# Two-layer graph network on one core: the first gathers' wait on the copy of x rows, the place of both layers' scatters behind the last gather, and layer 1's results in the own rows' places

## The chip, the cores and the metric

The kernel runs on one core of one Trainium2 chip. The metric is the device time of one execution in microseconds. The core has five engines: PE (matmul), DVE (vector work), ACT (scalar functions), POOL (here mostly the issuer of indirect DMAs) and SP (the issuer of most plain DMAs). Transfers themselves run on 16 DMA engines.

## The reference

A graph of N = 3327 nodes with F = 512 features each, all in f32. The adjacency matrix is symmetric with ones on the diagonal, and a row has some nine nonzeros on average (each pair is drawn at 0.0024). Both layers end in a residual and a layernorm.

```python
# layer 0: attention over neighbours, 4 heads of 128
feats = einsum('nf,hfo->hno', x, W)
logits = leaky_relu(e_self[:, :, None] + e_neigh[:, None, :], 0.2), masked by A
out0 = relu(concat over heads of softmax(logits) @ feats + b)
x = layernorm(x + out0)
# layer 1: two gated sums over the same neighbours
h = x @ W_sa;  s_left, s_right = h @ a_sa[:F], h @ a_sa[F:]
gate_a = sigmoid([A @ x, x] @ Wa.T + ba);  gate_b likewise with Wb
e = exp(-leaky_relu(s_left[:, None] + s_right[None, :], 0.01)) where A != 0, else 0
out1 = sigmoid(gate_a * (e / (sum(e) + 1e-5)) @ h + gate_b * (A @ (x @ W_g) + b_g))
x = layernorm(x + out1)
```

## The kernel before

The 3327 nodes are padded to 26 tiles of 128 rows. `sparse_pass` does not multiply by the adjacency matrix. It turns the matrix into lists of neighbours, sorts the nodes by their number of neighbours, and then fetches, for each tile, the neighbours' rows with indirect DMAs (a "gather": 128 rows of 2080 bytes, one row for each partition). A tile needs as many gathers as its longest list (the constant `CAPS`, 4 to 14), and nodes with still longer lists get an extra slot. The nodes form two groups: the first 12 tiles and the other 14. `gat_then_gated_gnn` calls `sparse_pass`, and after it a dense version that runs only if the graph doesn't fit the lists, which is not the case here.

**Up to about 200 us: lists and features.** The adjacency matrix comes in seven chunks on SP's queue (`load_adj`, L222). PE packs it into codes (L403), DVE takes the largest codes and decodes them (L71, L74, L442 to L479). Beside that, PE computes each tile's rows of features (L372), ACT copies them, and POOL sends them to a table in DRAM, `table0` (L384). The rows of the first group's nodes alternate in this table with their rows of x, so that one gather of double width gets a node's own features and its own x. These rows of x are copied into the table by one DMA of SP, `x_rows` (L238), which is put just ahead of the last adjacency chunk.

**About 200 to 632 us: layer 0, tile by tile.** `plan` writes down a tile's gathers in the list `waiting`, each with the number of slots handed out up to it. `gather` issues them on POOL (`indirect`, L616) from the head of that list as long as they fit into the `ring`, 42 slots of 128 rows in SBUF. `free(j)` gives a tile's slots back in program order. `at_first` issues, ahead of everything else, those gathers of the two tiles `early` that read features only (11 in all), and puts their two double-width gathers behind them. For each tile DVE and ACT then compute the softmax weights (`weigh_a`, L750 to L763, `weigh_b`, L777 to L779), DVE and ACT scale the gathered rows (L798, L796), and PE adds them up with a matmul by the identity (`attend`, L804). DVE adds the residual (`finish`, L883), the columns that layer 1 needs are worked out (L835, L839), and after each group of tiles `Norm` yields the layernorm's scale and shift. `publish` normalises a tile's row (ACT) and its columns (DVE, L846 and L847). It stays in SBUF as `row1(j)` and goes to the table of layer 1, `table1`: the first group's tiles by a plain DMA of SP (L849), the second group's by an indirect DMA of POOL (`put_rows`, which calls `scatter`, L146), since their order in DRAM is another one.

**About 632 to 1077 us: layer 1.** All gathers of layer 1 are planned at once, and a loop over the 26 tiles issues them by `gather` as slots come free. DVE computes weights (L1031 to L1061) and the weighted sum (`weighted`, L1096 and L1098), PE the plain sum (`plain_sum`, L1117), turns both (L1127) and multiplies them by the two weight matrices (`project`, L1136). Two steps later DVE forms the argument of the sigmoid in a buffer `za` (L1166), ACT takes its tanh (L1168), and DVE adds the residual `row1` (L1190). When `Norm` has a group (it ends at the tiles 3, 7, 11, 15, 19, 22, 24 and 25 of the order), ACT normalises its tiles in place (L1183) and POOL sends each to its place in the output (`scatter`, L146).

Instructions of one engine run in the order of the program. So a scatter that waits for ACT holds up the gathers behind it on POOL. A buffer of a pool with several copies (`bufs`) can be written again only once its last reader, a scatter's DMA among them, has finished. The framework derives all these waits from the regions that instructions read and write. Two helpers take a wait out: `declare_no_dep` opens a named group with one instruction in it, and `add_to_no_dep_group` adds an instruction to an existing group. `scatter` uses the groups `table1` and `out` so.

Of the kernel before, what the change touches and what calls it, by code (L numbers as in the profile page):

```python
# [8 lines left out]
F32 = mybir.dt.float32  # L9
AF = mybir.ActivationFunctionType  # L10
ALU = mybir.AluOpType
# [3 lines left out]
P = 128  # L15
# [20 lines left out]
GRP = 4  # L36
# [42 lines left out]
def sparse_pass(  # L79
# [39 lines left out]
    nc = tc.nc  # L119
    N, F = out.shape  # L120
# [23 lines left out]
    def scatter(group, dst, rows, src, last=None):  # L144

        put = nc.gpsimd.indirect_dma_start(  # L146
            out=dst, out_offset=bass.IndirectOffsetOnAxis(ap=rows, axis=0), in_=src, in_offset=None,
            bounds_check=last, oob_is_err=last is None,
        ).ins
        tc.declare_no_dep(put, group=group, reason="their rows are disjoint")  # L150
        tc.add_to_no_dep_group(group, put)
        nc.gpsimd.nop(nofuse=True)
# [23 lines left out]
    def place(j):  # L176

        return (0, j) if j < NG[0] else (1, j - NG[0])

    def own(j):  # L180
        g, i = place(j)
        return srt[g][:, i, 0:1]

    def row1(j):
        g, i = place(j)
        return x1[g][:, i, :]
# [22 lines left out]
    def load_x(i):  # L209
        if i < len(chunks):  # L210
            cw = min(CH, NP - chunks[i])
            xc = xcs[i] = pj.tile([P, KT, CH], F32, tag="xc", name=f"xc{i}", bufs=3)
            nc.sync.dma_start(xc[:, :, :cw], xB[i] if cw == CH else xL)
# [4 lines left out]
    def load_adj(i):  # L218
        cw = min(CH, NP - chunks[i])
        for q, (a, b) in enumerate(pairs_of(NT)):  # L220
            at = p0.tile([P, 2, CH], F32, tag="at", name=f"at{i}_{a}", bufs=AT)
            nc.sync.dma_start(at[:, :, :cw], adjB[i, q] if cw == CH else adjL[q])  # L222

            ones_of = at.bitcast(BF16).rearrange("p t (n w) -> p t n w", w=2)[:, :, :cw, 1]
            loaded[i, a], loaded[i, b] = ones_of[:, 0], ones_of[:, 1]
# [10 lines left out]
    for i in range(len(chunks)):  # L236
        if i == len(chunks) - 1:
            x_rows = nc.sync.dma_start(twos.rearrange("(n t) w -> n t w", t=2)[:, 0, :], xo[:N0]).ins  # L238
            tc.declare_no_dep(x_rows, group="x rows", reason="the first gathers read rows of features only")
        load_adj(i)  # L240
        load_x(i + 2)

# [370 lines left out]
    waiting, ends_at = [], {}  # L613

    def indirect(out_, table, ap):
        return nc.gpsimd.indirect_dma_start(  # L616
            out=out_, out_offset=None, in_=table, in_offset=bass.IndirectOffsetOnAxis(ap=ap, axis=0)
        ).ins
# [42 lines left out]
    def free(j):  # L661

        freed[0] = ends_at[j]
# [68 lines left out]
    first = list(range(NG[0]))  # L732
# [94 lines left out]
    def columns2a(j):  # L827
        xt1s[j] = m0.tile([P, KT, P], F32, tag="xt1", name=f"xt1_{j}")
        nc.scalar.copy(xt1s[j], turned[j])
# [8 lines left out]
    def columns3(j):  # L838
        nc.vector.tensor_copy(row1(j)[:, F : F + NCOL], turned[j])  # L839

    def publish(j, scale, shift):
        row = row1(j)[:, 0:F]
        nc.scalar.activation(row, row, AF.Identity, scale=scale, bias=shift)
        col = row1(j)[:, F : F + NCOL]
        t = m0.tile([P, NCOL], F32, tag="shifted", name=f"shifted{j}")
        nc.vector.scalar_tensor_tensor(t, v1sum, shift, bias8, ALU.mult, ALU.add)  # L846
        nc.vector.scalar_tensor_tensor(col, col, scale, t, ALU.mult, ALU.add)  # L847
        if j < NG[0]:
            put = nc.sync.dma_start(table1[j * P : (j + 1) * P, :], row1(j)).ins  # L849
            tc.add_to_no_dep_group("table1", put)  # L850
        else:
            rows_ready.append(j)
# [3 lines left out]
    def put_rows():  # L856
        for j in rows_ready:
            scatter("table1", table1[:, :], own(j), row1(j), N - 1)
        rows_ready.clear()
# [14 lines left out]
    def at_first():  # L874

        a, b = (CAPS[j] + 1 for j in early)
        waiting[: a + b] = waiting[1:a] + waiting[a + 1 : a + b] + [waiting[0], waiting[a]]
        for _ in range(a + b - 2):
            tc.add_to_no_dep_group("x rows", indirect(*waiting.pop(0)[1:]))

    def finish(j):
        y = row1(j)[:, 0:F]
# [64 lines left out]
    ready = [[], []]  # L947
    for i in range(NT + 3):
        for args in ready[0]:
            publish(*args)  # L950
        ready = [ready[1], []]
        third = order0[i - 2] if 2 <= i < NT + 2 else None
        if third is not None:
            columns2a(third)
        if 2 <= i < NT:
            attend(order0[i], i >= 3, lambda: third is None or columns2(third))
        elif third is not None:
            columns2(third)
        if 0 < i <= NT:
            j = order0[i - 1]  # L960
            y = row1(j)[:, 0:F]
            if i > 2:
                finish(j)
            put_rows()
            columns1(j)
            done = norm.add(i - 1, y)
            if done:
                k0, scale, shift = done
                ready[1] = [
                    (order0[k], scale[:, k - k0 : k - k0 + 1], shift[:, k - k0 : k - k0 + 1]) for k in range(k0, i)  # L970
                ]
        if i > NT:
            put_rows()
        if 2 <= i < NT + 2:
            columns3(order0[i - 2])
        if 0 < i <= 7:
            sort1(rankis[1], 2 * i - 2, 2 * i)
        if i == 8:
            climb(1, m0, psx.tile([P, B * H], F32, tag="pcol", name="climb1", bufs=2)[:, : B + H])
        if i == NG[0]:  # L980
            nc.vector.memset(over, 0.0)
            for j, c in enumerate(CAPS):
                if j in T0:
                    nc.vector.tensor_scalar(over[:, j, c:S], no_step, 0.0, None, ALU.is_lt)
                else:
                    nc.vector.memset(over[:, j, c:S], 1.0)
        if i == 3:
            nc.sync.dma_start(own1[:, 0, :], xo[N0:])
            nc.sync.dma_start(own1[:, 1, :], singles)
        if 2 <= i < NT - 1:  # L990
            weigh_a(order0[i + 1])
            weigh_b(order0[i + 1])
# [6 lines left out]
    m1 = ctx.enter_context(tc.tile_pool(name="m1", bufs=2))  # L999
# [8 lines left out]
    order, last, mid = by_len[2:7], by_len[:2][::-1], by_len[7:]  # L1008
# [7 lines left out]
    ew, gates, sums, plain, proj, zs, stair_sum = {}, {}, {}, {}, {}, {}, {}  # L1016
# [128 lines left out]
    weights_a(at_(0))  # L1145
    weights_b(at_(0))
    scaled_first(at_(0))
    ready = None
    for i in range(NT + 3):
        j, j1, jp, jpp = at_(i), at_(i + 1), at_(i - 1), at_(i - 2)  # L1150
        if i > 0 and jp is not None:
            free(jp)
        gather()
        if j1 is not None:
            own_score(j1)
        if jp is not None:
            sp = zs[jp, "sp"] = m1.tile([P, F], F32, tag="sp", name=f"sp{jp}")
            nc.scalar.activation(sp, plain[jp], AF.Copy, scale=gates[jp][:, 1:2])
            turn(jp, 0)
            turn(jp, 1)  # L1160
        if j is not None:
            plain_sum(j, False)
            weighted(j, 0)
        if jpp is not None:
            za = zs[jpp] = m1.tile([P, F], F32, tag="za", name=f"za{jpp}", bufs=GRP + 3)
            nc.vector.scalar_tensor_tensor(za, bias_g, gates[jpp][:, 1:2], proj[jpp], ALU.mult, ALU.add)  # L1166

            nc.scalar.activation(za, za, AF.Tanh, scale=0.5)  # L1168
        if jp is not None:
            project(jp, 0)  # L1170
        if j is not None:
            plain_sum(j, True)
        if j1 is not None:
            weights_a(j1)
        if j is not None:
            weighted(j, 1)
        if jp is not None:
            project(jp, 1)
        if ready:
            k0, scale, shift = ready  # L1180
            for k in range(k0, i - 2):
                z = zs[order[k]]
                nc.scalar.activation(  # L1183
                    z, z, AF.Identity, scale=scale[:, k - k0 : k - k0 + 1], bias=shift[:, k - k0 : k - k0 + 1]
                )
                scatter("out", out, own(order[k]), z, N - 1)
            ready = None
        if jpp is not None:
            za = zs[jpp]
            nc.vector.scalar_tensor_tensor(za, za, 0.5, row1(jpp)[:, 0:F], ALU.mult, ALU.add)  # L1190
        if j1 is not None:
            weights_b(j1)
            scaled_first(j1)
        if jpp is not None:
            ready = norm.add(i - 2, zs[jpp])
# [452 lines left out]
```

## Time and profile before

| What | us |
|---|---|
| Runs | 1079.59, 1087.12, 1090.84 |
| Median of the runs | 1087.12 |
| The profiled execution's own time | 1079.52 |
| Its span in the profile | 1077.4 |
| Last row of features sent by POOL | 157.63 |
| First gather of layer 0 issued | 177.22 |
| Last gather of layer 0 issued | 583.62 |
| Last scatter of layer 0 issued | 628.53 |
| Last gather of layer 1 issued | 994.68 |
| Last scatter of layer 1 issued | 1070.61 |

Times inside the profile are counted from the start of the span. A row of the costliest groups reads: line, engine, operation, output<-inputs and count, then busy time and mean ns of one, then the idle time that the engine had just before these instructions, with what ended most of it. The DMA_INDIRECT on POOL is the issue of a gather or scatter; the data lands later. A row of a timeline reads: start, duration, engine, line, operation, and in brackets the idle time before it with its releaser. A row of the waits reads: engine and line, what it waited for, then the total, the number of times, and the longest. A row of the windows gives, for each stretch, its length and each engine's busy time with its instructions, then the granted clock of PE, the share of the DMA engines and GB/s. "issue" is time in which the engine waited for nothing that the profile shows, "remote" a release by something that it can't name.

### The profile page before, as it was taken

Reading aid. Unit: us, or ns where it says so; the run is one execution under the profiler, and the core shown is the slowest. Engines: PE = TensorE matmul, PEld = TensorE weight load, DVE = VectorE, ACT = ScalarE, POOL = GpSimd, SP = SyncE. Lnnn points to the kernel's source line nnn. Section 1 sums busy time; section 2 is a strip of 40 time slices with the busy share of each in tenths; the row PEclk is TensorE's granted clock in tenths of the full one; section 3 lists DMA queues with packets and bytes.
Section 4 is the critical chain, followed back from the end, with each engine's and each line's share of the span. In section 5 each row is a group of like instructions: output and inputs, shape, how many; then the busy total and the mean of one; then the engine's idle time right before and its main releaser. Section 6 shows DMA issues by size and latency. Waiting matters only on the chain. (4 is left out here: it accounts for less than half of the span.)

```text
span 1077.4 us, 10335 instructions
## 1 busy us (share of the span) xinstructions
PE 823.0 (76%) x2518; PEld 431.5 (40%) x2518; DVE 735.3 (68%) x2100; ACT 288.8 (27%) x820; POOL 594.3 (55%) x641
## 2 busy tenths in 40 slices
PE   5698973053978887888588936289999969979994
PEld 4476751022434443434244412044444424434442
DVE  3486788137666676666448846069898986979983
ACT  1122210021333342434135511022223213222331
POOL 7511243752667666576755157755777777767101
PEclk9898995575997988888878967589999998989998
DMA  9999899982568677587765047745676675756101
GB/s 341 374 360 399 329 334 370 395 302 80 167 183 257 200 212 221 180 297 200 207 175 178 31 130 190 214 129 139 177 192 187 175 190 173 193 161 189 49 8 55
DMA packets 73349, 224.68 MB, mean 209 GB/s; under 512 B 12736, under 2 KB 16784, under 8 KB 72384
## 3 DMA queue, kind: packets, MB, share of 16 engines
q0 software_dynamic: 46368, 153.69, 48.2%
q1 hardware_dynamic: 24256, 68.13, 16.7%
q10 hardware_dynamic: 2656, 2.10, 0.6%
q8 instruction: 23, 0.38, 0.1%
q14 instruction: 46, 0.38, 0.1%
HBM read 203.02 MB, written 31.51 MB: 218 GB/s over the span
## 5 line engine op out<-in xcount | busy, mean ns | idle before, releaser
L616 POOL DMA_INDIRECT ring<-table,srt x464 | 475.4, 1025 | 247.7 <-issue 109.3
L804 PE MATMUL acc<-ring,ident 128*128 128x512 f32 x504 | 262.9, 669 | 90.3 <-DMA ring<-table,srt 33.7
L804 PEld LDWEIGHTS acc<-ring,ident 128*128 128x128 f32 x504 | 102.1, 213 | 215.2 <-issue 146.3
L1096 DVE SCALAR_TENSOR_TENSOR sw<-ring,e,sw 128x512 f32<-128x512 f32 x226 | 169.4, 750 | 12.7 <-ACT sw L1080 7.2
L1117 PE MATMUL acc<-ring,ident 128*128 128x512 f32 x264 | 126.7, 615 | 12.8 <-DMA ring<-table,srt 9.6
L1136 PE MATMUL po<-wsa,sT 128*128 128x512 f32 x208 | 100.0, 627 | 32.0 <-issue 29.1
L372 PE MATMUL pf<-w,xc 128*128 128x260 f32 x416 | 106.0, 419 | 13.1 <-DVE w L312 13.1
L798 DVE TENSOR_TENSOR ring<-ring,w 128x512 f32<-128x512 f32 x176 | 111.3, 691 | 0.5
L372 PEld LDWEIGHTS pf<-w,xc 128*128 128x128 f32 x416 | 86.4, 210 | 30.2 <-DVE w L312 13.8
L1136 PE MATMUL po<-wg,sT 128*128 128x512 f32 x208 | 93.7, 593 | 0.0
L796 ACT ACTIVATE ring<-ring,w 128x128 f32<-128x128 f32 x304 | 91.6, 390 | 0.9 <-issue 0.9
L1117 PEld LDWEIGHTS acc<-ring,ident 128*128 128x128 f32 x264 | 51.7, 197 | 82.0 <-issue 56.9
L1136 PEld LDWEIGHTS po<-wsa,sT 128*128 128x128 f32 x208 | 41.7, 202 | 88.6 <-issue 82.6
L146 POOL DMA_INDIRECT out<-za,srt x26 | 29.1, 1118 | 78.8 <-ACT za L1183 74.6
L1098 DVE TENSOR_TENSOR ring<-ring 128x512 f32<-128x512 f32 x94 | 65.0, 691 | 3.2
L763 ACT ACTIVATE w<-w 128x40 f32<-128x40 f32 (+10 forms) x26 | 6.2, 237 | 212.5 <-DVE w L762 113.6
L384 POOL DMA_DIRECT2D table<-row x26 | 14.3, 549 | 87.4 <-ACT st L381 84.7
L1129 ACT COPY sT<-pt 128x512 f32<-128x512 f32 x52 | 28.5, 588 | 117.9 <-PE pt L1127 57.0
L1136 PEld LDWEIGHTS po<-wg,sT 128*128 128x128 f32 x208 | 39.4, 190 | 48.8 <-issue 47.8
L403 PE MATMUL pc<-at,pow 128*32 128x512 bf16 (+1 forms) x182 | 24.4, 414 | 39.7 <-DMA at<-in_adjB 24.9
L1166 DVE SCALAR_TENSOR_TENSOR za<-bias_g,gate,po 128x512 f32<-128x512 f32 x26 | 19.3, 742 | 38.6 <-remote 29.2
L376 ACT COPY row<-pf 128x512 f32<-128x512 f32 x26 | 15.2, 586 | 97.7 <-issue 49.2
(253 smaller groups left out, 949.9 us busy)
## 6 DMA issues: line engine op xcount, KB each, us to landing
at<-in_adjB SPq DMA_DIRECT2D x78, 512.0 KB
ring<-table,srt POOLq DMA_INDIRECT x464
table<-row POOLq DMA_DIRECT2D x26, 260.0 KB
xc<-in_xB SPq DMA_DIRECT2D x6, 1024.0 KB
own<-in_xo SPq DMA_DIRECT2D x1, 3640.0 KB
own<-table SPq DMA_DIRECT2D x1, 3640.0 KB
at<-in_adjL SPq DMA_DIRECT2D x13, 256.0 KB
table<-in_xo SPq DMA_DIRECT2D x1, 3120.0 KB
```

The lines of the kernel that those rows point to most:

```text
L146: put = nc.gpsimd.indirect_dma_start(out=dst, out_offset=bass.IndirectOffsetOnAxis(ap=rows, axis=0), in_=src, in_offset=None, bounds_check ...
L372: nc.tensor.matmul(pf[:, hh, :HC], xc[:, k, o : o + P], w0[:, k, hh, :], start=(k == 0), stop=(k == KT - 1))
L403: nc.tensor.matmul(pc[32 * c : 32 * c + 32, : nt * P], pow2[:, s, :], loaded[i, m], start=(s == 0), stop=(m + 1 not in ms or s == 3),)
L616: return nc.gpsimd.indirect_dma_start(out=out_, out_offset=None, in_=table, in_offset=bass.IndirectOffsetOnAxis(ap=ap, axis=0)).ins
L796: nc.scalar.activation(gv[:, h, :], gv[:, h, :], AF.Copy, scale=w[:, s, h : h + 1])
L798: nc.vector.tensor_tensor(gv, gv, w[:, s, :].rearrange("p (h o) -> p h o", o=1).to_broadcast([P, H, FO]), ALU.mult)
L804: nc.tensor.matmul(acc, ident, row, start=(lean and s == 0), stop=(s == CAPS[j] and j not in T0))
L1096: nc.vector.scalar_tensor_tensor(sw, g[:, i, 0:F], e[:, s : s + 1], sw, ALU.mult, ALU.add)
L1098: nc.vector.tensor_add(g[:, i, 0:F], g[:, i - 1, 0:F], g[:, i, 0:F])
L1117: nc.tensor.matmul(plain[j], to, row, start=(not sums_of_two and i == 0), stop=(sums_of_two and i == len(rows) - 1),)
L1129: nc.scalar.copy(sT, pt)
L1136: nc.tensor.matmul(proj[j], sT[:, k, :], wt[:, k, :], start=(half + k == 0), stop=(half + k == KT))
```

## The change

There are three parts.

The copy of x rows and the first gathers change their roles in the group `x rows`: each of the 11 gathers of `at_first` is now declared itself, and `x_rows` is added to the group. In the program as compiled before, the first gather waits for the copy `x_rows`. In the program as compiled after, the first gather waits for the rows of features and for a word written into them earlier, and the wait for `x_rows` stands at the twelfth gather, the first of double width.

In layer 0, `put_rows` is called inside the loop only when `waiting` is empty, so when all gathers of layer 0 have been issued. Four of the 14 scatters stood ahead of further gathers before; now all 14 stand behind the last one.

In layer 1, the residual (L1190) writes its result into `row1(j)`, where it read the residual from, and no longer into `za`. ACT normalises it there, and the scatter reads it there. The pool of `za` has three buffers instead of seven. The scatters are collected in a list `outs` and issued once `waiting` is empty. Before, 16 of the 26 stood ahead of further gathers; now all stand behind the last one. The number of instructions is the same on each engine.

```diff
--- before.py
+++ after.py
@@ -236,7 +236,7 @@
     for i in range(len(chunks)):
         if i == len(chunks) - 1:
             x_rows = nc.sync.dma_start(twos.rearrange("(n t) w -> n t w", t=2)[:, 0, :], xo[:N0]).ins
-            tc.declare_no_dep(x_rows, group="x rows", reason="the first gathers read rows of features only")
+            tc.add_to_no_dep_group("x rows", x_rows)
         load_adj(i)
         load_x(i + 2)
 
@@ -876,7 +876,7 @@
         a, b = (CAPS[j] + 1 for j in early)
         waiting[: a + b] = waiting[1:a] + waiting[a + 1 : a + b] + [waiting[0], waiting[a]]
         for _ in range(a + b - 2):
-            tc.add_to_no_dep_group("x rows", indirect(*waiting.pop(0)[1:]))
+            tc.declare_no_dep(indirect(*waiting.pop(0)[1:]), group="x rows", reason="they read rows of features only")
 
     def finish(j):
         y = row1(j)[:, 0:F]
@@ -961,7 +961,8 @@
             y = row1(j)[:, 0:F]
             if i > 2:
                 finish(j)
-            put_rows()
+            if not waiting:
+                put_rows()
             columns1(j)
             done = norm.add(i - 1, y)
             if done:
@@ -1145,7 +1146,7 @@
     weights_a(at_(0))
     weights_b(at_(0))
     scaled_first(at_(0))
-    ready = None
+    ready, outs = None, []
     for i in range(NT + 3):
         j, j1, jp, jpp = at_(i), at_(i + 1), at_(i - 1), at_(i - 2)
         if i > 0 and jp is not None:
@@ -1162,7 +1163,7 @@
             plain_sum(j, False)
             weighted(j, 0)
         if jpp is not None:
-            za = zs[jpp] = m1.tile([P, F], F32, tag="za", name=f"za{jpp}", bufs=GRP + 3)
+            za = zs[jpp] = m1.tile([P, F], F32, tag="za", name=f"za{jpp}", bufs=3)
             nc.vector.scalar_tensor_tensor(za, bias_g, gates[jpp][:, 1:2], proj[jpp], ALU.mult, ALU.add)
 
             nc.scalar.activation(za, za, AF.Tanh, scale=0.5)
@@ -1179,15 +1180,18 @@
         if ready:
             k0, scale, shift = ready
             for k in range(k0, i - 2):
-                z = zs[order[k]]
+                z = row1(order[k])[:, 0:F]
                 nc.scalar.activation(
                     z, z, AF.Identity, scale=scale[:, k - k0 : k - k0 + 1], bias=shift[:, k - k0 : k - k0 + 1]
                 )
-                scatter("out", out, own(order[k]), z, N - 1)
+                outs.append((own(order[k]), z))
             ready = None
+        while outs and not waiting:
+            scatter("out", out, *outs.pop(0), N - 1)
         if jpp is not None:
             za = zs[jpp]
-            nc.vector.scalar_tensor_tensor(za, za, 0.5, row1(jpp)[:, 0:F], ALU.mult, ALU.add)
+            zs[jpp] = row1(jpp)[:, 0:F]
+            nc.vector.scalar_tensor_tensor(zs[jpp], za, 0.5, zs[jpp], ALU.mult, ALU.add)
         if j1 is not None:
             weights_b(j1)
             scaled_first(j1)
```

## The prediction

> **What bounds the kernel now.** I read the page first (engine totals, chain, costliest groups), then each engine's waits, then windows by stage, and last the timelines of POOL and DVE around the places that the change touches.
>
> ```profile
> span 1077.4 us, 10335 instructions
> PE 823.0 (76%) x2518; PEld 431.5 (40%) x2518; DVE 735.3 (68%) x2100; ACT 288.8 (27%) x820; POOL 594.3 (55%) x641
> issue 11%; DVE 10%; PE 8%; DMA 4%; POOL 3%; another core or an unknown queue 3%; ACT 2%; POOLq 0%; DVEq 0%
> L616 POOL DMA_INDIRECT ring<-table,srt x464 | 475.4, 1025 | 247.7 <-issue 109.3
> L146 POOL DMA_INDIRECT out<-za,srt x26 | 29.1, 1118 | 78.8 <-ACT za L1183 74.6
> ```
>
> No engine is full over the whole span. POOL, whose queue the change rearranges, is busy for 55%, and its gathers (L616) are preceded by 247.7 us of idle time: it has room. The windows by stage say what fills each:
>
> ```profile
> core 0: us, PE busy (x) PEld busy (x) DVE busy (x) ACT busy (x) POOL busy (x), PEclk, DMA share, GB/s
> 150.00:205.00 55.00, 21.26 (x100) 10.65 (x98) 37.87 (x170) 3.07 (x10) 23.55 (x27) 0.60 1.04 377
> 260.00:632.00 372.00, 302.14 (x842) 150.00 (x842) 243.06 (x712) 141.08 (x418) 215.02 (x216) 0.85 0.61 185
> 660.00:700.00 40.00, 11.10 (x26) 4.89 (x24) 7.33 (x14) 1.49 (x3) 30.25 (x33) 0.66 0.75 208
> 700.00:800.00 100.00, 94.54 (x257) 45.40 (x258) 83.15 (x184) 27.71 (x68) 63.99 (x59) 0.95 0.56 157
> 900.00:1000.00 100.00, 92.51 (x249) 43.51 (x248) 89.06 (x185) 25.59 (x65) 71.66 (x66) 0.95 0.63 176
> ```
>
> Layer 0 (260 to 632) is PE work (81%), layer 1 (700 to 1000) PE and DVE together (94% and 83%, then 93% and 89%). Before 205 the DMA engines are full. The stretch 660 to 700 is odd: PE, DVE and ACT nearly stand still while POOL issues gathers.
>
> Then the question that decides this change: does anybody wait for a gather? Among DVE's waits over the whole span, one row is for the ring that the gathers fill:
>
> ```profile
> DVE za L1166 <- remote: 29.2, 2, 24.9
> DVE e L1031 <- DMA ring<-table,srt: 12.2, 2, 11.5
> ```
>
> The 11.5 us is the start of layer 1 (at 641 us), which waits for layer 0's last scatter at 628.5, itself waiting for DVE. In DVE's waits from 660 to 1000 no row names the ring. Taking each gather's issue against its first reader in the timelines, I find its data landed 15 us or more ahead in layer 0, and 20 us or more in layer 1 from its fourth tile on.
>
> **What the Trainium skill says.** "Perfetto Trace Analysis", DMA Instruction — SWDGE (GPSIMD), says that the recorded end of a GpSimd DMA is the end of its descriptor generation, not of the transfer. The trace agrees: a gather is recorded with 0.95 us, and its landing follows 3 to 4 us after its issue. So a POOL row prices POOL's queue only. "DMA: Bandwidth & Descriptors", Issuing engines are not separate DMA queues, says that all issuers share the 16 DMA engines. It agrees too: from 150 to 205 us, where SP's copies and POOL's gathers overlap, the share is 1.04 at 377 GB/s, so moving gathers into that stretch moves bytes ahead of other bytes. "SBUF — State Buffer", SBUF: two separate sides, says that GpSimd can be kept from writing descriptors while DVE works in its two-port mode. The trace fits in kind: a gather takes 0.95 us while DVE idles (178 to 182) and 1.08 to 1.21 while it is busy (988 to 996).
>
> **The change part by part.** Every engine keeps its number of instructions; only positions and waits change.
>
> *The first 11 gathers.* Now:
>
> ```profile
> 157.63 0.54 POOL L384 DMA_DIRECT2D table<-row  x1 [3.03 <-ACT st L381]
> 177.22 1.00 POOL L616 DMA_INDIRECT ring<-table,srt  x1 [19.05 <-DMA at<-in_adjL]
> 178.52 0.96 POOL L616 DMA_INDIRECT ring<-table,srt  x1 [0.30 <-issue]
> 203.38 0.18 DVE L750 TENSOR_TENSOR w<-ring,srt 128x24 f32<-128x24 f32 x1 [0.43 <-DMA ring<-table,srt]
> ```
>
> In the compiled order the first gather's wait is on the copy of x rows (L238, issued at 157.17, 3.1 MB); the name in brackets is another transfer on the same queue. After the change it waits for the rows of features, the last written from 157.63 and quiet by about 164. So 11 gathers, 11 x 1.25 = 13.8 us of POOL, move from 177-191 to about 164-178; the twelfth takes over the wait for x rows. But their reader, DVE, is busy with the decoding of a chunk of adjacency until 202.9 and waited 0.43 us: that is all there is to gain, and POOL then fills its 42 slots earlier and waits longer. Cost side: 11 x 266 KB = 2.9 MB go ahead of x rows and the last adjacency chunk, 2.9 MB / 0.4 MB per us = 7 us. PE's use of that chunk (176.84 to 189.7) slips by up to 7, but what it feeds is used by ACT only at 226 and by DVE at 241, and in between PE stands idle for 33.7 us. Bounds -0.4 to +7; I take -0.4.
>
> *Layer 0's scatters.* Four of 14 (522.37 to 527.60) move behind the last gather (583.62): 4 x 1.31 = 5.2 us. The gathers behind 522 run 5.2 us earlier, and all had 15 us and more in hand: 0. At the new place POOL idles 21.6 us before the scatter at 611.4 (for DVE L846), which covers the four. The last scatter still follows DVE's last group: 0. Were that cover gone, it would be +5.2.
>
> *Layer 1's scatters.* 16 of 26 stand between gathers (763.9, 828.1, 896.1, 957.8, four each); they take 16 x about 1.42 = 23 us of POOL, and POOL waits some 9 us there for ACT (L1183). So 32 us go from the stream of gathers. No DVE or PE wait ends with a gather there: 0. They come back behind the last gather:
>
> ```profile
> 994.68 1.15 POOL L616 DMA_INDIRECT ring<-table,srt  x1 [0.30 <-issue]
> 1015.49 1.02 POOL L146 DMA_INDIRECT out<-za,srt  x1 [19.65 <-ACT za L1183]
> 1048.44 0.98 POOL L146 DMA_INDIRECT out<-za,srt  x1 [27.35 <-ACT za L1183]
> 1070.61 0.98 POOL L146 DMA_INDIRECT out<-za,srt  x1 [2.08 <-ACT za L1183]
> ```
>
> From 996.1, 16 x 1.3 to 1.5 = 21 to 24 us: done at 1017 to 1020, then the group of 1015.49 until about 1025, and 23 us of idle time are left before 1048. If the last gather comes earlier, there is more room. The scatter that ends the kernel still waits for ACT's last group. Without that cover, the whole 23 us would be at the end.
>
> *Rows in place, three za buffers.* The same instructions with another output. The tanh and L1166 lose a wait for an old scatter that never showed; L1190 and L1183 gain one on the copy of those rows into the table, landed over 130 us earlier. Nobody queues behind either: 0.
>
> Sum: -0.4 us, for which I take -1 (POOL a little less in DVE's way). The profiled execution took 1079.5 us, 2.1 above its span, and would become 1078.5; the median of the runs lies 7.6 above it, so 1087.1 - 1 = 1086.
>
> **What the sum leaves open.** There are stretches where PE, DVE and ACT nearly stop without a waited-for producer, and in all of them POOL issues gathers without a pause and the DMA share is high:
>
> ```profile
> 516.00:545.00 29.00, 12.89 (x34) 6.23 (x34) 8.90 (x21) 6.54 (x22) 19.28 (x20) 0.73 0.68 199
> 545.00:600.00 55.00, 49.49 (x140) 24.67 (x140) 39.20 (x116) 23.32 (x71) 28.46 (x29) 0.89 0.53 156
> 662.00:703.00 41.00, 9.10 (x21) 4.05 (x19) 7.04 (x13) 1.10 (x4) 30.58 (x32) 0.63 0.75 209
> 874.00:895.00 21.00, 10.19 (x21) 4.39 (x20) 12.38 (x35) 2.68 (x9) 14.75 (x15) 0.76 0.73 198
> ```
>
> Each costs PE its length less its work at the usual rate (49.49/55 = 0.90, in layer 1 0.945): 29 - 12.89/0.90 = 14.7 us; 41 - 9.10/0.945 = 31 us; 21 - 10.19/0.945 = 10.2 us. The trace doesn't say why. The change alters POOL's pattern around the first and the last, so these are the unknown of the forecast.
>
> **Rivals.**
>
> *Faster: the stalls at 516 and 874 go.* POOL falls behind at the scatters (and waits there for ACT), then catches up in a dense run of gathers; with the scatters away it stays at its ring's limit and the dense runs vanish. For it: four scatters at 522 lie inside a stall, and 874-895 lies between two groups. Against: the first stall began at 516, before its scatters. Gain up to 14.7 + 10.2 = 25, likely 20: 1067.
>
> *Slower: a longer unbroken run of gathers.* The stall of 662 ended as POOL paused (702). Scatters waiting for ACT are pauses too (1.7, 2.8 and 4.4 us above the usual 0.3); without them POOL runs on until the ring stops it, and one or two further stalls of the size at 874 appear in 760-990. The burst of 16 scatters could be another such run. For it: POOL was never idle in any stall. Against: the ring of 42 bounds POOL's lead. From one stall of 10.2 us it decides; at one and a half, +15: 1102.
>
> *Slower, small: the early gathers delay x rows and the last chunk* by their 7 us, if the start of layer 0 follows transfers rather than DVE: 1093. Against: PE's 33.7 us of idle time behind that chunk.
>
> *That the change does nothing it says* is out: the compiled order has the new wait and the scatters in one row.
>
> **How the numbers follow.** Covered everywhere, 1086: 0.42. Stalls gone, 1067: 0.33. Further stalls, 1102: 0.17. Delayed copies, 1093: 0.08. One per cent is 10.9 us, about what a measurement of this kernel can tell from no change. The first case spreads some 6 us each way and lies within it, and so does the delayed copy for the most part; of the stalls' cases a small share stays within. So faster 0.33, same 0.47, slower 0.20. The range takes 20 us below and 18 above: 1066 to 1104; the likeliest case's own is 1080 to 1092.
>
> **What would show it.** Right: first gather at about 164, DVE's first weights still near 203; fourteen table scatters behind 584; from about 970 to 996 on a row of 16 or more scatters without a wait, then those of the late groups after ACT; the last scatter ending the chain; and the three stalls at about their lengths. Wrong: a DVE or PE wait on the ring between 660 and 1000, the last table scatter well off 628, the last group's ACT ready before POOL is free, or a stall of 10 us or more that has come or gone.

## The result, and the profile after

In the first comparison the kernel after took 1067.61 us (median of 4 runs, 1062.41 to 1073.25) against 1088.98 us for the kernel before. The ratio is 0.9875, with a 95% interval of 0.9834 to 0.9915: faster by 1.25%. The profiled execution took 1068.62 us with a span of 1066.8. It is 10.9 us below the profiled execution of the kernel before (1079.52), while the medians lie 21.4 us apart: the two profiles can account for half of the gain only.

The experiments ran in later comparisons, on two chips where the same kernel before takes 940 to 942 us, not 1089, a difference that nothing in the program explains and that carries most of the answer.

The page of the kernel after, engine totals and POOL's gathers, has the same work as before:

```profile
span 1066.8 us, 10313 instructions
PE 814.2 (76%) x2518; PEld 426.4 (40%) x2518; DVE 735.3 (69%) x2100; ACT 289.0 (27%) x820; POOL 593.5 (56%) x641
L616 POOL DMA_INDIRECT ring<-table,srt x464 | 475.2, 1024 | 265.1 <-issue 98.8
```

DVE's busy time is the same (735.3 us), and POOL has more idle time ahead of its gathers than before (265.1 against 247.7 us), not less. PE's 2518 instructions are busy for 8.8 us less (814.2 against 823.0); the rest of the difference is waiting. Here is POOL at the start of layer 0, from the timeline of the kernel after (the first and the twelfth gather):

```profile
164.35 1.00 POOL L616 DMA_INDIRECT ring<-table,srt  x1 [6.48 <-DMA at<-in_adjB]
186.56 0.94 POOL L616 DMA_INDIRECT ring<-table,srt  x1 [8.72 <-DMA table<-in_xo]
```

And DVE in the same stretch, with the first weights and the first two results of layer 0:

```profile
193.89 0.18 DVE L750 TENSOR_TENSOR w<-ring,srt 128x24 f32<-128x24 f32 x1 [2.24 <-DMA at<-in_adjL]
229.22 0.69 DVE L883 SCALAR_TENSOR_TENSOR x1a<-acc,x1a 128x512 f32<-128x512 f32 x1 [26.09 <-remote]
240.57 0.69 DVE L883 SCALAR_TENSOR_TENSOR x1a<-acc,x1a 128x512 f32<-128x512 f32 x1 [10.66 <-remote]
```

The first gather goes out at 164.35 instead of 177.22, and the twelfth takes over the wait for the copy of x rows (186.56). DVE's first weights come 9.5 us earlier. All of that is lost 35 us later: the second result of layer 0 ends at 241.26 us, before at 241.56. DVE waits 26 us for a signal that the profile names only as remote.

The names of such waits need a caution. The two profiles of the first comparison lack many records of signals. From 160 us on, the profile of the kernel before holds 5489 semaphore updates, and the later profile of the same kernel (shown below) holds 11738, while both hold the same 10335 instructions and 73349 DMA packets. So their lists of DMA issues differ: the first gives no time from issue to landing for the gathers, and the second gives a median of 3.9 us:

```profile
ring<-table,srt POOLq DMA_INDIRECT x464
ring<-table,srt POOLq DMA_INDIRECT x464, 3.9
```

In the profiles of the first comparison, "remote" and "issue" can therefore mean that the record of the signal is missing, and the absence of a row for the ring is weak evidence that nobody waits for it. The tables and windows here rest on the starts and durations of the instructions, and of those both profiles have the same number.

The windows of the three stretches in which the engines nearly stood still before, now of the kernel after:

```profile
516.00:545.00 29.00, 24.66 (x69) 12.13 (x68) 17.20 (x45) 12.45 (x35) 20.09 (x21) 0.90 0.74 212
662.00:703.00 41.00, 19.95 (x45) 8.30 (x43) 15.59 (x29) 3.99 (x11) 31.55 (x32) 0.75 0.75 203
874.00:895.00 21.00, 20.33 (x60) 9.71 (x60) 18.62 (x37) 7.29 (x15) 16.43 (x16) 1.00 0.73 194
```

PE's busy time there is 24.66, 19.95 and 20.33 us, where it was 12.89, 9.10 and 10.19. (The windows are fixed in time, so they do not hold exactly the same work.) The second stretch is the most telling: no edit changes the order of instructions between 632 and 703 us, and it still changed. Setting the end of each tile's last addition side by side (L883 in layer 0; L1190 before and L1194 after in layer 1) gives where the 12.7 us between the two profiles lie:

| Point | before | after | difference |
|---|---|---|---|
| layer 0, result 2 of 26 | 241.56 | 241.26 | -0.3 |
| layer 0, result 18 | 514.94 | 524.13 | +9.2 |
| layer 0, result 19 | 538.52 | 536.50 | -2.0 |
| layer 0, result 26 | 621.21 | 622.74 | +1.5 |
| layer 1, result 1 | 709.61 | 687.78 | -21.8 |
| layer 1, result 2 | 719.65 | 712.90 | -6.8 |
| layer 1, result 12 | 872.69 | 869.58 | -3.1 |
| layer 1, result 13 | 895.55 | 884.65 | -10.9 |
| layer 1, result 26 | 1066.01 | 1053.31 | -12.7 |
| end of the span | 1077.4 | 1066.8 | -10.6 |

The 11.2 us at the stall of 516 had nearly been lost before it (+9.2 by result 18, most of it behind result 12 at 423 us). At the start of layer 1, 23.3 us were won (from +1.5 to -21.8) and 15.0 lost at once. The stall at 874 brought 7.8. At the very end 2.1 us were given back.

### The profile page after: what moved, and what is told of

Same layout as the page of the kernel before. It is cut to its first block, busy times and chain, and to the rows that moved or that the text cites. A ratio compares the mean times of both kernels' runs of the same rounds, so it can differ in the third digit from the quotient of the medians.

```text
span 1066.8 us, 10313 instructions
## 1 busy us (share of the span) xinstructions
PE 814.2 (76%) x2518; PEld 426.4 (40%) x2518; DVE 735.3 (69%) x2100; ACT 289.0 (27%) x820; POOL 593.5 (56%) x641
## 2 busy tenths in 40 slices
DMA packets 73349, 224.68 MB, mean 211 GB/s; under 512 B 12736, under 2 KB 16784, under 8 KB 72384
## 5 line engine op out<-in xcount | busy, mean ns | idle before, releaser
L616 POOL DMA_INDIRECT ring<-table,srt x464 | 475.2, 1024 | 265.1 <-issue 98.8
L829 ACT COPY xt<-x1t 128x512 f32<-128x512 f32 x26 | 15.2, 584 | 94.9 <-remote 39.2
L835 PEld LDWEIGHTS pcol<-v,xt 128*128 128x128 f32 x208 | 33.1, 228 | 17.3 <-issue 14.1
```

Source lines behind the costliest of these rows:

```text
L616: return nc.gpsimd.indirect_dma_start(out=out_, out_offset=None, in_=table, in_offset=bass.IndirectOffsetOnAxis(ap=ap, axis=0)).ins
L835: nc.tensor.matmul(pcol, xt1[:, k, :], v1[:, k, :], start=(k == 0), stop=(k == KT - 1))
```

## The experiments

**The single parts.** Part one alone swaps the roles of `x_rows` and the first gathers. Its edit, then what was expected:

```diff
-            tc.declare_no_dep(x_rows, group="x rows", ...)
+            tc.add_to_no_dep_group("x rows", x_rows)
...
-            tc.add_to_no_dep_group("x rows", indirect(*waiting.pop(0)[1:]))
+            tc.declare_no_dep(indirect(*waiting.pop(0)[1:]), group="x rows", ...)
```

> Part one of the change alone (the first 11 gathers don't wait for the copy of x rows). Theory of the stalls (the gain of the whole change is stalls that moved or went, and no part removed a wait on the path): first DVE weights near 194 us instead of 203, but the second result of layer 0 (DVE L883) still near 241, since both wait for PE's signals that come only when the stall ends; total within 6 us of before, either way. Theory of the wait (the copy of x rows held layer 0 up): second result of layer 0 by 10 us earlier, total 8 to 13 us lower.

Measured: 942.79 against 941.02 us, ratio 1.0017 (0.9994 to 1.0039). The theory of the wait falls: in these executions freeing the first gathers is worth nothing that can be seen.

Part two alone holds back the table's scatters:

```diff
-            put_rows()
+            if not waiting:
+                put_rows()
```

> Part two alone (four scatters of layer 0 behind its last gather). Theory of the stalls: the stall at 516 to 545 moves or goes (up to 15 us), the last result of layer 0 stays within 3 us of 621, because later stalls of layer 0 take it back; total within 6 us of before. Theory of the freed stream (POOL's queue free of scatters gives the time): about 0 to -3 us here, since only 5.2 us of POOL's stream are freed.

Measured: 933.91 us, ratio 0.9917 (0.9889 to 0.9946), so about 7 us faster. Neither theory had that: the theory of the stalls allowed 6 us either way, the other 3. It came back in a later comparison (expected there as follows) with 934.33 us, ratio 0.9925 (0.9895 to 0.9954).

> Part two alone once more, beside the others. On a chip where before takes 941 us: -6 to -7 us (ratio 0.993), 1 to 3 us below the kernel after. On a chip where before takes 1088 us: no late gathers, so the part gains nothing of its own, and any difference is in the stalls.

Part three alone takes the hunks on `za`, `outs` and `row1` of the diff:

> Part three alone (layer 1's scatters behind its last gather, results in the own rows' places, three buffers for za). Theory of the freed stream: nearly all of the gain, -10 to -14 us, and no stall before the scatter groups' old places at 874 to 895 and 939 to 955; the stall at 662 to 703 as long as before (31 us), as no scatter stood there. Theory of the stalls: the same two stalls gone, -8 to -14 us, but with new ones elsewhere possible, so -14 to +5 us.

Measured: 941.73 us, ratio 1.0012 (0.9992 to 1.0032). Nothing, so the theory of the freed stream falls for layer 1. The stalls cannot be seen in this run either, for a reason that the next experiment shows.

**Both kernels again.** The kernel before was run once more for its profile, and the kernel after beside it.

> The kernel before once more, for its profile beside the runs of this chip. If the chip is like that of the single parts (941 us): no stretch of over 10 us in layers 0 and 1 where PE and DVE both stand below half, apart from the hand-over between the layers; DVE waits some 10 us for gathers between 440 and 540 us, as in the runs of part one and part three alone. If it is like that of the first comparison (1088 us): the stalls at 188, 516, 662 and 874 us are back, at the same places if the kernel's order fixes them, at others if they are an accident of each execution.

> The kernel after once more. Theory of the late gathers (the four scatters of layer 0 stood ahead of gathers that were late on the faster chip, and the other parts move nothing there): -7 us, as part two alone (0.8%), on a chip with 941 us; on a chip with 1088 us about -13 us as in the first comparison, since there the gathers have 15 us in hand and the gain is in the stalls. Theory of additive parts with a cost of part one or three: between -7 and -3 us.

Before took 941.32 us (against 941.48, ratio 1.0002), after 937.12 us, ratio 0.9951 (0.9935 to 0.9967). Windows of this profile of the kernel before, over the same stretches:

```profile
516.00:545.00 29.00, 21.52 (x78) 12.23 (x78) 23.84 (x85) 13.31 (x33) 13.51 (x12) 0.88 0.36 131
662.00:703.00 41.00, 39.35 (x111) 18.50 (x110) 38.54 (x89) 10.22 (x26) 31.86 (x31) 1.00 0.68 193
874.00:895.00 21.00, 18.46 (x48) 7.97 (x47) 19.15 (x42) 7.19 (x18) 12.17 (x12) 1.00 0.53 161
```

At 662 to 703 PE works 39.35 of 41 us, while POOL issues without a pause (31.86 us busy, 31 issues, four of them scatters). So a dense run of gathers does not by itself stall the others, and the stalls are not written into the program: the span of the same kernel is 138 us shorter here, 1077.4 against 939.5. About 37 us of that is PE's busy time (823.0 against 785.8), the rest is PE's waiting. What makes one execution stall and another not stays open; no run here met the stalls again.

Without stalls layer 0 ends at 535.5 us instead of 621.2, and now gathers are late. DVE's waits from 440 to 540 us, of the kernel before in this later comparison:

```profile
DVE w L750 <- DMA ring<-table,srt: 4.5, 4, 1.9
DVE w L750 <- issue: 3.6, 1, 3.6
```

That is 8.1 us, where some 10 were expected for such an execution.

The same view of part two alone:

```profile
DVE w L750 <- DMA ring<-table,srt: 0.5, 1, 0.5
```

And the same on DVE's timeline, three tiles' weights of the kernel before:

```profile
478.22 0.20 DVE L750 TENSOR_TENSOR w<-ring,srt 128x44 f32<-128x44 f32 x1 [0.75 <-DMA ring<-table,srt]
489.00 0.20 DVE L750 TENSOR_TENSOR w<-ring,srt 128x36 f32<-128x36 f32 x1 [1.39 <-DMA ring<-table,srt]
502.12 0.20 DVE L750 TENSOR_TENSOR w<-ring,srt 128x40 f32<-128x40 f32 x1 [3.59 <-issue]
```

The same three of part two alone:

```profile
476.89 0.20 DVE L750 TENSOR_TENSOR w<-ring,srt 128x44 f32<-128x44 f32 x1
486.38 0.20 DVE L750 TENSOR_TENSOR w<-ring,srt 128x36 f32<-128x36 f32 x1
496.76 0.20 DVE L750 TENSOR_TENSOR w<-ring,srt 128x40 f32<-128x40 f32 x1 [0.20 <-DMA ring<-own,srt]
```

In the first three rows nearly every tile waits, 0.75, 1.39 and 3.59 us ("issue" at the last is a wait whose releaser the profile does not name). In the second three the waits are gone, and the distance to the kernel before grows from 1.3 to 5.4 us. From there on it stays at 6 to 7 us to the end of layer 1. In the second run of part two DVE still waits 3.0 us for the ring there, and layer 0 ends just as early.

The end of layer 0 (its last L883) sorts all twelve later profiles. With the four scatters ahead of the last gathers it comes at 535.5, 536.4 and 536.5 us (before, part one, part three); in the eight with part two and nothing in the scatters' place it comes between 528.0 and 530.1. The means lie 6.9 us apart. From the first of the four scatters to the gather behind them POOL's queue passes 5.7 us in before and in part one, and 6.3 in part three. The twelfth profile is that of the next experiment.

**POOL's time or the scatters' traffic?** To tell these apart, part two was kept, and at the place of the four scatters POOL computed for a while instead:

```diff
             if not waiting:
                 put_rows()
+            elif rows_ready and not paused:
+                paused.append(1)
+                for k in range(11):
+                    nc.gpsimd.tensor_tensor(pause, bias0[:, :192], bias0[:, :192], ALU.mult)
```

> Part two alone, and at the place that the four scatters left in layer 0, eleven POOL multiplications of 128 x 192 numbers into a tile that nobody reads: by the 1.26 us that a 128 x 512 one takes, 0.47 us each, so some 5.2 us of POOL without any DMA. Theory of the late gathers (POOL's time ahead of gathers that are already late is the whole of part two's gain): the gain is gone, within 2 us of before, and DVE again waits some 6 to 10 us for gathers at the end of layer 0. If it was the scatters' traffic or their writes into the table: the gain stays, -6 us.

Measured: 944.66 us, ratio 1.0047 (1.0028 to 1.0066). The eleven operations took more than planned. POOL's group of them in this run:

```profile
L970 POOL TENSOR_TENSOR pause<-bias 128x192 f32<-128x192 f32 x11 | 7.9, 717 | 0.8
```

DVE's waits from 440 to 540 us in the same run:

```profile
DVE w L750 <- DMA ring<-table,srt: 9.7, 5, 3.5
```

They occupy POOL for 7.9 + 0.8 = 8.7 us, against 5.7 to 6.3 for the scatters. The waits for gathers are back, and layer 0 ends 9.0 us later than with part two alone (538.20 against 529.22). The loss shows as waits for gathers (9.7 us of the ring against 0.5). 8.7 us of POOL without any DMA cost 9 us, so POOL's time ahead of late gathers is enough to explain the loss, about one for one. The scatters' 6.9 us for 5.7 to 6.3 us of POOL leave about a microsecond at most for their traffic.

**What part three does.** With parts two and three, and with parts one and two:

> Parts two and three together, without part one. Theory of the late gathers: the same as part two alone and as the kernel after, within 2 us (-7 us at 941). If part one costs something (2.9 MB of gathers ahead of the copies): 2 to 4 us better than after.

> Parts one and two, layer 1 as before. Theory: part one gains and costs nothing on top, total within 1.5 us of part two alone and the end of the kernel 11.4 us after the last residual; 2 us below the kernel after. If part one's early 2.9 MB cost something: 1 to 3 us above part two alone from the first tiles on.

Measured: 935.86 us, ratio 0.9942 (0.9921 to 0.9962), and 936.77 us, ratio 0.9946 (0.9924 to 0.9968). Both overlap with each other, with the kernel after (0.9951) and with part two alone (0.9917 and 0.9925). That part one costs 1 to 3 us on top can be neither shown nor excluded.

The profiles show one thing about part three more sharply than the times. From the last residual addition to the end of the span it takes 11.4 us in before, in part one, in part two and in both together, and 13.4 to 13.7 us in all profiles with the late scatters of layer 1. POOL's last rows, first of the kernel after in the later comparison:

```profile
L1585 POOLq COMPARE_BRANCH  x1: 53/53/53, 927.3 to 927.3; - x1
L1585 POOLq EVENT_SEMAPHORE  x1: 17/17/17, 930.0 to 930.0; - x1
L1649 POOLq DRAIN  x3: 50/103/4970, 930.1 to 935.6; - x3
```

To see which half of part three does it, part two was run with the results in the own rows' places and three `za` buffers, but with layer 1's scatters left between the gathers:

```diff
-                z = zs[order[k]]
+                z = row1(order[k])[:, 0:F]
...
-            nc.vector.scalar_tensor_tensor(za, za, 0.5, row1(jpp)[:, 0:F], ALU.mult, ALU.add)
+            zs[jpp] = row1(jpp)[:, 0:F]
+            nc.vector.scalar_tensor_tensor(zs[jpp], za, 0.5, zs[jpp], ALU.mult, ALU.add)
```

> Parts two and the half of three that keeps results in the own rows' places with three za buffers; layer 1's scatters stay between the gathers. Theory that the own rows' tiles, kept in use until the last output has landed, put POOL's closing drain (5.0 us) behind that landing: end of the last residual to end of kernel 13.4 us as in the kernel after, 2 us more than with part two alone, total 2 us above part two alone. If the late scatters make the longer end: 11.4 us and a total equal to part two alone.

The expected theory falls. The run took 932.52 us, ratio 0.9913 (0.9889 to 0.9937), and the distance is 11.4 us:

```profile
L1583 POOLq COMPARE_BRANCH  x1: 50/50/50, 927.0 to 927.0; - x1
L1583 POOLq EVENT_SEMAPHORE  x1: 17/17/17, 927.5 to 927.5; - x1
L1647 POOLq DRAIN  x3: 50/109/5048, 927.5 to 933.2; - x3
```

In both, POOL ends with a drain of about 5 us (the last number of its row's durations). With the late scatters POOL's first instruction behind the branch around the dense version comes 2.7 us after the branch instead of 0.5, and the drain starts that much later. Why the late scatters make POOL slow at this branch was not tried further; ACT and DVE take 2.5 to 3 us at the same branch in these two profiles, but nothing long follows there.

**Two attempts to go further.** The copies that fill the second group's double rows compete with the first gathers, so they were moved to ACT's queue, where they go out later:

```diff
-            nc.sync.dma_start(own1[:, 0, :], xo[N0:])
-            nc.sync.dma_start(own1[:, 1, :], singles)
+            nc.scalar.dma_start(own1[:, 0, :], xo[N0:])
+            nc.scalar.dma_start(own1[:, 1, :], singles)
```

> The kernel after, with the two copies into the double-width rows of the second group (SP, 3.6 MB each, issued at 190 and 191 us, first read after 425 us) moved to ACT's queue, where the program has them (about 300 us). If the stall of 203 to 240 comes from full DMA engines: it goes, the second result of layer 0 comes at about 220 instead of 241, and the total falls by 15 to 20 us against after. If it comes from POOL's unbroken gathers: the second result stays at 235 to 242, and the total within 5 us of after.

Measured: 936.23 us, ratio 0.9946 (0.9929 to 0.9962), as the kernel after has without it. The two copies went out at 266 us. The second result of layer 0 came at 218.1 us, as in part one alone (217.8). There was no stall at 203 to 240 us to remove in these comparisons, so the question that it was built for stays open.

The other attempt went at layer 1's own late gathers, on top of part two:

```diff
     order += last
+    order[5:9] = order[6], order[5], order[8], order[7]
```

> Part two alone, and in layer 1's order the two tiles of 7 gathers each moved one place ahead of the tiles of 13 and 14 gathers (places 5 to 8). In the runs of part two alone DVE still waits 5 to 7 us for the gathers of the 13-gather tile, whose data lands 0.1 us before its use, and later tiles have 5 us and more in hand. Theory of the late gathers, here in layer 1: that wait falls to under 2 us and the total by 3 to 6 us against part two alone, to about 929 us (ratio 0.987). If the wait only goes to the 14-gather tile behind it: no gain, ratio 0.992.

Measured: 936.94 us, ratio 0.9941 (0.992 to 0.9962), so no gain. DVE's wait for the 13-gather tile did fall from 6.5 us (580 to 640 us in the second run of part two) to 0.9, but the seventh result, behind both tiles of the exchange, came 4.5 us later than with part two alone. DVE's waits for PE between 530 and 940 us grew instead (L1168 for the projection from 5.7 to 8.0 us, L1035 for `to_nodes` from 0.3 to 4.0). Neither expectation had that.

## Why the prediction was right or wrong

The range of 1066 to 1104 us held 1067.61, at its lower edge, and the likeliest case (1086, no change) was not what happened. The value of the rival "the stalls at 516 and 874 go" (1067) was met, but not its reasons. That the range held is in part luck.

*The working of the parts, in the first comparison.* It held in the main. The first gather came at 164.35 (said: about 164), 14 table scatters stood behind layer 0's last gather and 20 output scatters in one row behind layer 1's, and no DVE wait for the ring of more than 0.5 us appeared in layer 0's second half, and none from 700 to 1000 us. "DVE's first weights still near 203" was wrong: they came at 193.89, because DVE decoded without interruption and was done at 191.6 instead of 202.9. In the kernel before, nine waits of 0.8 to 2.2 us stand in this decoding between 188 and 203 us, 11.3 us in all and most of them behind DVE's own preceding instruction (one is shown in the last section). The prediction took these waits for work. The step behind it held all the same, since the gain was gone at 241 us. PE's work on the last chunk slipped by 9.5 us (176.84 to 186.38) where 7 was the estimate.

*The step that failed: the price of the stalls' movement in the likeliest case.* The prediction took the stalls at about their lengths, zero net. The table above shows a net -12.7 us at the last result, and its large steps lie at these stretches. Of the rival's two terms, the 14.7 us at 516 measured 11.2, of which 9.2 had been lost ahead of it; the 10.2 us at 874 measured 7.8. The largest term, the stall at 662, was held unchanged by every case, and there 23.3 us went and 15.0 came back. So the rival's mechanism, scatters away and no dense catching up, is not shown: POOL issued as densely at 662 to 703 in the kernel after (31.55 us busy) as before, and in the later comparisons such dense runs stalled nobody. Whether the change removes stalls in such executions, or they fall differently in every one, cannot be said: there is one profile of each kernel, and no experiment met the stalls again.

*The step that held only by the stalls' grace: "all had 15 us and more in hand: 0".* This was right for the trace that it was read from, and wrong as a statement about the kernel. It can be counted without the records of signals, from each gather's issue, 3.9 us to its landing, and the start of its first reader. In the kernel before of the first comparison, the last five tiles of layer 0 have 20.8 us or more in hand. In the later profile of the same kernel four of these five have 0.5 us or less. The slack came with the stalls, in which PE and DVE stood still and POOL went on issuing. Without them layer 0 ends 86 us earlier, and the four scatters' 5.7 us of POOL come out at 6 to 7 us. The prediction named the price if the cover is gone, +5.2, but for the new place behind the last gather, not for the old one.

*Layer 1's scatters: 0.* Right, and with a reason that can be seen. In the later comparisons a tile's last gather, counted in the same way, landed less than 1 us ahead of its first reader at place 23 of 26 in the kernel before, and 22 us ahead with part three. The freed stream, 22 us in this profile where the prediction read 32 from its own, became slack that no one needed. What was missed is +2.1 us at the end, behind the scatter that the prediction took as the end of its chain.

The whole, where it can be taken apart: 1.0017 x 0.9917 x 1.0012 = 0.9946, and the kernel after measured 0.9951. There the change is part two, less the 2 us of part three's ending. The first comparison gained 0.8% more. The half of that gain that its profiles cover lies at the stalls, whose cause stays open. Part two alone, with or without the in-place half of part three, has the lowest times here (932.5 to 934.3 us); its distance to the kernel after is within the intervals.

## What to carry to other kernels

Slack that is read from a trace belongs to that execution: where engines stand still for reasons that the program doesn't contain, every prefetch looks early. Before pricing an edit at zero for its slack, compute the slack that is left if the unexplained stalls are taken out, and price the edit for both. On this queue of in-order DMA issues, what stood ahead of late gathers cost about its own time, whether scatters (6.9 us for about 6) or arithmetic (9.0 for 8.7); ahead of early ones, 22 us of scatters cost nothing that could be measured (ratio 1.0012). And before a missing row is read as "nobody waits", see whether the profile has the records that would show the wait.

## What the hardware showed that was not expected

The same kernel took 1089 us in the first comparison and 941 in later ones on two chips, with PE's mean granted clock at 0.855 and 0.910 in the two profiles. In the long executions, instructions start late behind the work that they follow. In the kernel after, PE's matmuls for the first tile of layer 0 are recorded from 205.1 to 212 us, and DVE's L883, which follows them, waits until 229.22 for "remote". In the later comparison the same instruction started at 213.20, released by PE in the usual way. It even happens inside one engine. Here is one step of DVE's decoding in the kernel before, first in the first comparison, then in the later one:

```profile
199.88 0.28 DVE L475 SCALAR_TENSOR_TENSOR some<-low,some 128x96 f32<-128x96 int32 x1 [1.13 <-DVE low L474]
189.72 0.26 DVE L475 SCALAR_TENSOR_TENSOR some<-low,some 128x96 f32<-128x96 int32 x1
```

In the first row DVE stands idle for 1.13 us behind its own preceding instruction; in the second it goes on at once. That these executions also lack records of signals may have the same cause or another; no run shows which. That the recording itself held the engines up is not excluded either.

POOL's small operations cost more than in proportion to their size. The eleven multiplications of 128 x 192 numbers took 507 to 836 ns each, 717 on average, with DVE working for 8.52 of 8.70 us beside them. A 128 x 512 one early in the kernel took 1262, so the estimate in proportion (470) was a third too low. Whether DVE's work or a fixed part of each operation makes the difference was not separated. The issue of a gather is longer beside a working DVE as well: in the kernel before of the first comparison it takes 1.09 us on average where DVE works for 90% of it or more (257 gathers), and 0.95 us where DVE works for less than a tenth of it (106).
